# A graph network's attention stage: one-hots made by ScalarE, exponentials kept in PSUM, and sorting steps that read one half from PSUM

## Chip, core and metric

The kernel runs on one core of a Trainium2 chip. The metric is the device time of a run in microseconds, as the median of three runs; beside it stands one execution recorded by the hardware profiler. VectorE is called DVE in the profile, ScalarE ACT, GpSimd POOL, TensorE PE (with PEld for its weight loads) and SyncE SP.

## The reference

A graph has N = 12500 nodes with 128 features and E = 200000 edges, sorted by destination. Two layers follow one another: an edge-biased attention over each node's incoming edges, and three graph convolutions with batch norm.

```python
h = jnp.maximum(_layernorm(x, axis=-1), 0.0)
# attention, 8 heads of 16
q = (x @ Wq.T).reshape(N, H, C); k = ...; v = ...
scores = jnp.einsum('ehc,ehc->eh', q[dst], k[src]) / np.sqrt(C) + edge_attr @ We.T
seg_max = jax.ops.segment_max(scores, dst, num_segments=N)
ex = jnp.exp(scores - seg_max[dst])
denom = jax.ops.segment_sum(ex, dst, num_segments=N)
out = jax.ops.segment_sum(v[src] * (ex / denom[dst])[:, :, None], dst, num_segments=N)
...
x = x + out
h = jnp.maximum(_layernorm(x, axis=-1), 0.0)
# three times: h @ W, gather by src, times norm, segment_sum by dst, batch norm
x = x + graph_convolutions(h, src, dst)
```

## The kernel before, in words

A prologue normalises x, multiplies it by the three attention weights and writes q and the joined k and v rows to HBM tables (`q_d`, `kv_d`). A flag then chooses between a general path and `fast`, which runs here.

**Attention** (L885 to L1130) works on 106 tiles of 118 destination nodes. Each tile has a window of WE = 2048 edges, laid out as 128 partitions by JJ = 16. For each tile:

- 16 indirect DMAs of POOL (`gather`, L147, called for `kv`, with three buffers from pool `ga`) fetch the k and v rows of 128 edges each.
- A one-hot `oht` [128, 2048] (L1013, VectorE) compares the edges' local destinations with the partition number. TensorE multiplies its columns by `qt`, so that each edge gets its q row in PSUM (`qe`, L1019). VectorE multiplies by k (L1020, in four parts) and sums over each head (L1023).
- TensorE transposes the edge attributes (`et_p`, copied to `et` by ACT) and adds their bias (`sm`, L1036). Four scans (L1051, L1053, each twice), two scans across partitions (L1067, L1069) and small matmuls (L1058 to L1072) give each edge the maximum of its segment.
- ACT writes the exponentials into column C of `vals` in SBUF (L1081). VectorE multiplies the v rows by them (L1082).
- A second one-hot `oh` [128, 16, 118] (`one_hot`, L675 to L677, VectorE) serves as weights of the 16 matmuls that sum by destination into `acc` (L1089), which ACT copies out (L1090).

**Placing.** Between these parts runs a generator, `place_edges` (L680), which prepares the convolutions' layout. It sorts 106 rows of 2048 keys twice by a bitonic network. Each sort has 66 steps; each step is one minimum (L701) and one maximum (L702) over 1024 pairs, from one SBUF tile `A` to the other. Between and after the sorts stand other VectorE instructions over rows of up to 2048 elements (ranks, shifts by bits, masks). The generator stops at each `yield`. `go_on(1)` is called four times in a tile (L1025, L1063, L1073, L1084), so four stages of the generator are issued in each tile, from the group of tiles in which all edges have been loaded (tile 24) on. What is left is run after the last tile (L1129).

The lines above are the order in which the program is written. A scheduler then puts the instructions of each engine into one fixed queue, so that parts of two or three neighbouring tiles alternate. In the queue each instruction waits for its semaphores, and everything behind it waits too. The PSUM pools are `ps2` with two buffers (`qe`, `acc`) and `ps1` with one (`nb`, `et_p`, `sm`, `ends`): eight banks in all.

**Convolutions** (L1160 to L1400) come after attention. They use the placed layout: rows are taken from SBUF by one-hot matmuls, and the rest is gathered by POOL (`rows`).

Of the kernel before, what the change touches and what calls it, by code (L numbers as in the profile page):

```python
# [8 lines left out]
FP = mybir.dt.float32  # L9
BF = mybir.dt.bfloat16  # L10
I32 = mybir.dt.int32
AF = mybir.ActivationFunctionType
# [5 lines left out]
P = 128  # L18
D = 128
H = 8  # L20
# [28 lines left out]
def tile_gnn(ctx: ExitStack, tc: tile.TileContext, x, src, dst, ea, wqkvT, weT, w1, w2, w3, par, out):  # L49
# [608 lines left out]
    def fast():  # L658
# [16 lines left out]
        def one_hot(oh, dl):  # L675
            sh = list(oh.shape)
            nc.vector.tensor_tensor(oh, iota_f[:sh[0], :TN].unsqueeze(1).to_broadcast(sh),  # L677
                                    dl.unsqueeze(2).to_broadcast(sh), op=ALU.is_equal)

        def place_edges(rt, ps):  # L680
# [19 lines left out]
            def swap(lo, hi, lo2, hi2):  # L700
                nc.vector.tensor_tensor(lo2, lo, hi, op=ALU.min)  # L701
                nc.vector.tensor_tensor(hi2, lo, hi, op=ALU.max)  # L702

            def sort(turn):
                size = 2
                while size <= WE:
                    a, b = (x.rearrange("t (n z) -> t n z", z=size) for x in (A[turn], A[1 - turn]))
                    h = size // 2
                    swap(a[:, :, :h], a[:, :, h:][:, :, ::-1], b[:, :, :h], b[:, :, h:][:, :, ::-1])
                    yield  # L710
                    turn = 1 - turn
                    d = h // 2
                    while d:
                        a, b = (x.rearrange("t (n w d) -> t n w d", w=2, d=d) for x in (A[turn], A[1 - turn]))
                        swap(a[:, :, 0], a[:, :, 1], b[:, :, 0], b[:, :, 1])
                        yield
# [42 lines left out]
            nc.vector.tensor_scalar(sm[:, 3:4], sm[:, 2:3], float(OV), None, op0=ALU.is_gt)  # L759
            mb = ps.tile([P, 2, MG], FP, name="nb")  # L760
            nc.tensor.matmul(mb[0:1, 0, 0:1], sm[:, 3:4], ones[:NTT, 0:1], start=True, stop=True)
            yield
            nc.vector.tensor_scalar(slotted, mb[0:1, 0, 0:1], 0.0, None, op0=ALU.is_equal)

# [120 lines left out]
        with ExitStack() as s:  # L885
# [9 lines left out]
            ps2 = s.enter_context(tc.tile_pool(name="ps2", bufs=2, space=PSUM))  # L895
            ps1 = s.enter_context(tc.tile_pool(name="ps1", bufs=1, space=PSUM))

            wbd = once.tile([P, 4 * H], FP, name="wbd")
# [12 lines left out]
            nc.vector.tensor_scalar(shift[:, 0], iota_f, pid[:, 1:2], None, op0=ALU.is_equal)  # L911
            nc.vector.tensor_scalar(shift[:, 1], iota_f, pid[:, 2:3], None, op0=ALU.is_equal)
            NV = 2
            vals = [once.tile([P, JJ, H * (C + 1) + 1], FP, name=f"vals{i}") for i in range(NV)]
# [45 lines left out]
            def go_on(n):  # L960
                for _ in range(n if steps else 0):
                    next(steps, None)

            loaded = 0
            for t0 in range(0, NTT, NG):
                n = min(NG, NTT - t0)
                if t0 % MG == 0:
# [16 lines left out]
                    nc.vector.tensor_scalar(lf[:, 1, :mn], dw[:, :mn, 0], N + 1.0, None, op0=ALU.add)  # L984
                    nb = ps1.tile([P, 2, MG], FP, name="nb")
                    for k in range(2):
# [11 lines left out]
                for t in range(t0, t0 + n):  # L998
# [13 lines left out]
                    oht = wk.tile([P, WE], FP, name="oht")  # L1012
                    nc.vector.tensor_scalar(oht, dw_b, iota_q, None, op0=ALU.is_equal)  # L1013
                    ohv = oht.rearrange("a (p j) -> a p j", j=JJ)
                    qk = kv[:, :, :D]
                    for j in range(0, JJ, 4):
                        qe = ps2.tile([P, 4, D], FP, name="qe")
                        for k in range(4):
# [5 lines left out]
                                            qk.rearrange("p j (h c) -> p j h c", h=H), AX.X, ALU.add)  # L1024
                    go_on(1)  # L1025

# [45 lines left out]
                    nc.tensor.matmul(far[:, 1, :], r[:, 1, 1:], ident[:H, :H], start=True, stop=True)  # L1072
                    go_on(1)  # L1073
                    for k, j in ((0, 0), (1, JJ - 1)):
# [5 lines left out]
                    vh = va[:, :, :H * (C + 1)].rearrange("p j (h c) -> p j h c", h=H)  # L1080
                    nc.scalar.activation(vh[:, :, :, C], mx.rearrange("p h j -> p j h"), AF.Exp)  # L1081
                    nc.vector.tensor_tensor(vh[:, :, :, :C], kv[:, :, D:].rearrange("p j (h c) -> p j h c", h=H),  # L1082
                                            vh[:, :, :, C:].to_broadcast([P, JJ, H, C]), op=ALU.mult)
                    go_on(1)  # L1084
# [365 lines left out]
```

## Time and profile before

| what | value |
|---|---|
| median of three timed runs | 7355.95 us (7324.02 to 7399.03) |
| the profiled execution's own time | 6154.56 us |
| its span, first to last instruction | 6152.8 us |
| mean granted TensorE clock | 0.796 |
| busy: PE, PEld | 4406.0 (72%), 4115.5 (67%) us |
| busy: DVE, ACT, POOL | 3396.2 (55%), 1011.7 (16%), 4084.2 (66%) us |
| first and last gather of `kv` | about 148 and 2931 us |
| first and last sorting instruction (L701, L702) | about 744 and 1728 us |
| last placing instruction (L873) | about 2495 us |

A row of an instruction group reads: line, engine, operation, output<-inputs, count | busy us, mean ns of one | idle time of the engine just before them, and what ended it. "issue" means that nothing visible in the profile was waited for. A row of windows reads: start:end in us, length, then the busy time and count of PE, PEld, DVE, ACT and POOL, the granted clock, the DMA share and GB/s. A row of the timeline reads: start, length in us, engine, line, operation.

### The profile page before, as it was taken

The page shows a single profiled execution, that of the slowest core. Times are in us where ns is not written, and L with a number is a line of the kernel's source. Part 1 is how long each engine was busy: PE and PEld are TensorE (multiplying, and loading weights), DVE is VectorE, ACT ScalarE, POOL GpSimd, SP SyncE. Part 2 cuts the span into 40 slices and gives each one's busy share as a digit, 9 for nine tenths or more (in the row PEclk, how much of TensorE's full clock was granted, in tenths as well). Part 3 has the DMA queues.
Part 4 walks back from the last instruction along what each step waited for, and adds up shares of the span by engine and source line. Part 5 has one row for each costly group of instructions (what it writes and reads, how often), then busy time and mean ns, then how long its engine had stood idle before and what let it go on. Part 6 is the DMA issues. An engine that isn't in the chain of part 4 may idle for free. (4 is left out here: it accounts for less than half of the span.)

```text
span 6152.8 us, 80384 instructions
## 1 busy us (share of the span) xinstructions
PE 4406.0 (72%) x28564; PEld 4115.5 (67%) x28564; DVE 3396.2 (55%) x5972; ACT 1011.7 (16%) x2374; POOL 4084.2 (66%) x3617
## 2 busy tenths in 40 slices
PE   6676666666666665767487787877787787778777
PEld 2666655555566665666377777777777776777777
DVE  7566688887876677655243343353343344434344
ACT  3111111110111111111112122111121211112120
POOL 0777788888888888777266566636666664666663
PEclk9677766666676776767788888898888888888888
DMA  6555544433444444454588888878888887888888
GB/s 188 152 143 138 137 112 106 113 103 109 105 128 120 122 112 112 131 132 114 150 214 216 218 216 218 213 209 217 219 216 221 213 211 204 219 219 219 221 215 209
DMA packets 607714, 1051.07 MB, mean 171 GB/s; under 512 B 191227, under 2 KB 418491, under 8 KB 607201
## 3 DMA queue, kind: packets, MB, share of 16 engines
q1 hardware_dynamic: 464311, 695.85, 41.5%
q0 software_dynamic: 142608, 348.39, 23.9%
q8 instruction: 232, 3.80, 0.3%
q14 instruction: 175, 1.43, 0.1%
q10 hardware_dynamic: 388, 1.60, 0.1%
HBM read 773.19 MB, written 272.26 MB: 170 GB/s over the span
## 5 line engine op out<-in xcount | busy, mean ns | idle before, releaser
L148 POOL DMA_INDIRECT rows<-t_d,srcO x1908 | 1827.6, 958 | 1329.2 <-issue 560.2
L148 POOL DMA_INDIRECT kv<-kv_d,srcA x1696 | 2252.3, 1328 | 536.7 <-issue 484.3
L1249 DVE TENSOR_TENSOR oh<-nums,dlS 128x1888 f32<-128x1888 f32 x318 | 674.3, 2121 | 1527.2 <-PE zp L1255 1517.9
L1253 PE MATMUL zp<-oh,mr 128*128 128x118 f32 x6360 | 966.6, 319 | 567.5 <-DMA mr<-m 440.4
L1253 PEld LDWEIGHTS zp<-oh,mr 128*128 128x128 f32 x6360 | 925.5, 233 | 586.4 <-DMA mr<-m 348.7
L1019 PE MATMUL qe<-qt,oht 128*128 128x128 f32 x3392 | 841.4, 415 | 247.3 <-DVE kv L1020 110.7
L1224 PE MATMUL gp<-hs,go 128*117 128x128 f32 x7056 | 891.8, 281 | 125.8 <-DVE go L1221 69.8
L1019 PEld LDWEIGHTS qe<-qt,oht 128*128 128x128 f32 x3392 | 767.1, 310 | 289.7 <-issue 166.8
L1224 PEld LDWEIGHTS gp<-hs,go 128*117 128x117 f32 x7056 | 831.9, 184 | 165.1 <-issue 117.1
L1226 ACT COPY stage<-gp 117x512 f32<-117x512 f32 x1008 | 521.8, 532 | 1375.0 <-PE gp L1224 936.8
L1020 DVE TENSOR_TENSOR kv<-qe,kv 128x512 f32<-128x512 f32 x424 | 289.4, 685 | 678.8 <-DMA kv<-kv_d,srcA 536.8
L1089 PE MATMUL acc<-vals,oh 128*118 128x137 f32 x3392 | 539.8, 329 | 150.5 <-DVE vals L1082 150.0
L1089 PEld LDWEIGHTS acc<-vals,oh 128*118 128x118 f32 x3392 | 522.1, 225 | 171.6 <-DVE vals L1082 171.3
L1221 DVE TENSOR_SCALAR go<-gi,iota_q 128x468 f32<-128x468 uint8 x1008 | 427.8, 456 | 224.5 <-DMA gi<-gi_d 111.8
L1255 PE MATMUL zp<-oh,rows 128*128 128x118 f32 x3816 | 513.2, 288 | 0.2 <-DMA rows<-t_d,srcO 0.2
L1255 PEld LDWEIGHTS zp<-oh,rows 128*128 128x128 f32 x3816 | 492.2, 206 | 0.4 <-DMA rows<-t_d,srcO 0.4
L1058 PE MATMUL ends<-ident,mg 128*8 128x128 f32 x212 | 53.0, 343 | 344.4 <-DVE mg L1053 305.6
L1082 DVE TENSOR_TENSOR vals<-kv,vals 128x2048 f32<-128x2048 f32 x106 | 242.3, 2286 | 27.2 <-ACT vals L1081 26.8
L1058 PEld LDWEIGHTS ends<-ident,mg 128*8 128x8 f32 x212 | 11.7, 96 | 366.1 <-DVE mg L1053 298.8
L1023 DVE TENSOR_REDUCE sc<-kv 128x128 f32<-128x2048 f32 x106 | 240.8, 2272 | 0.0
L677 DVE TENSOR_TENSOR oh<-iota_f,dlA 128x1888 f32<-128x1888 f32 x106 | 224.0, 2113 | 5.0 <-PE acc L1089 5.0
L1036 PE MATMUL sm<-wbd,et 128*128 128x32 f32 x848 | 167.8, 351 | 45.0 <-DVE mg L1075 37.7
(242 smaller groups left out, 3648.1 us busy)
## 6 DMA issues: line engine op xcount, KB each, us to landing
m<-stage SPq DMA_DIRECT2D x252, 784.0 KB
mr<-m SPq DMA_DIRECT2D x318, 560.0 KB
dw_b<-dlb_d SPq DMA_DIRECT2D x106, 512.0 KB
gi<-gi_d SPq DMA_DIRECT2D x252, 204.8 KB
rows<-t_d,srcO POOLq DMA_INDIRECT x1908
kv<-kv_d,srcA POOLq DMA_INDIRECT x1696
ebx<-in_edge_attr_dram SPq DMA_DIRECT2D x106, 256.0 KB
mr<-m SPq DMA_DIRECT2D x318, 75.0 KB
```

What stands on the lines that cost most here:

```text
L148: nc.gpsimd.indirect_dma_start(out=o, out_offset=None, in_=table[:, :], in_offset=bass.IndirectOffsetOnAxis(ap=idx, axis=0))
L1019: nc.tensor.matmul(qe[:, k, :], ohv[:, :, j + k], qt, start=True, stop=True)
L1020: nc.vector.tensor_tensor(qk[:, j:j + 4, :], qe, qk[:, j:j + 4, :], op=ALU.mult)
L1023: nc.vector.tensor_reduce(sc.rearrange("p h j -> p j h"), qk.rearrange("p j (h c) -> p j h c", h=H), AX.X, ALU.add)
L1082: nc.vector.tensor_tensor(vh[:, :, :, :C], kv[:, :, D:].rearrange("p j (h c) -> p j h c", h=H), vh[:, :, :, C:].to_broadcast([P, JJ, H, C] ...
L1089: nc.tensor.matmul(acc, oh[:, j, :], va[:, j, :], start=(j == 0), stop=(j == JJ - 1))
L1221: nc.vector.tensor_scalar(go[:, :n], gv[:, a:a + n], iota_q, None, op0=ALU.is_equal)
L1224: nc.tensor.matmul(gp[:, i, :], go[:, i].rearrange("p t k -> p (t k)"), hs[:, g * SG + a + i, :], start=True, stop=True)
L1226: nc.scalar.copy(stage[:, a:a + n, :], gp[:, :n, :])
L1249: nc.vector.tensor_tensor(oh, nums.unsqueeze(1).to_broadcast(sh), dlS[:, t, :].unsqueeze(2).to_broadcast(sh), op=ALU.is_equal)
L1253: nc.tensor.matmul(zp[:, i, :], mr[:q, j, :], oh[:q, j, :], start=False, stop=False)
L1255: nc.tensor.matmul(zp[:, i, :], rows[:, j, :], oh[:, RC + j, :], start=False, stop=(j == JO - 1))
```

## The change

Five edits, all in attention and the placing that runs with it:

- `oht` and `oh` are made by ACT: Abs of the difference, then Relu(1 - x), which gives 1 where the difference is zero. `oh` takes one Abs for each of the 16 columns, because the bias is a value per partition.
- The exponentials go to PSUM (`ex`, a part of `sm`). VectorE's product reads them there, and ACT copies them to column C of `vals`.
- Each sorting step is cut in two halves. For each, ACT copies the upper elements to a PSUM bank (`hc`, one buffer), and after a `yield` the minimum and the maximum read them there.
- `go_on(2)` in place of `go_on(1)`, at all four places.
- PSUM: `sm` now has two buffers and also serves `nb`; `acc` has one and also serves the placing's `mb`; `hc` takes the bank that is free.

```diff
             def swap(lo, hi, lo2, hi2):
-                nc.vector.tensor_tensor(lo2, lo, hi, op=ALU.min)
-                nc.vector.tensor_tensor(hi2, lo, hi, op=ALU.max)
+                n, d = lo.shape[1:]
+                for k in range(2):
+                    cut = (slice(None), slice(k * n // 2, (k + 1) * n // 2)) if n > 1 else (
+                        slice(None), slice(None), slice(k * d // 2, (k + 1) * d // 2))
+                    hc = ps.tile([P, WE // 4], FP, name="hc")[:NTT].rearrange(
+                        "t (n d) -> t n d", n=max(1, n // 2))
+                    nc.scalar.copy(hc, hi[cut])
+                    yield
+                    nc.vector.tensor_tensor(lo2[cut], lo[cut], hc, op=ALU.min)
+                    nc.vector.tensor_tensor(hi2[cut], lo[cut], hc, op=ALU.max)
...
-                    swap(a[:, :, :h], a[:, :, h:][:, :, ::-1], b[:, :, :h], b[:, :, h:][:, :, ::-1])
-                    yield
+                    yield from swap(a[:, :, :h], a[:, :, h:][:, :, ::-1], b[:, :, :h], b[:, :, h:][:, :, ::-1])
...
-            mb = ps.tile([P, 2, MG], FP, name="nb")
+            mb = ps.tile([TN, H * (C + 1) + 1], FP, name="acc")
...
+            shared = [P, 2 * JJ + 2, H]
...
+            niota = once.tile([P, 1], FP, name="niota")
+            nc.vector.tensor_scalar(niota, iota_q, -1.0, None, op0=ALU.mult)
+
+            def where_zero(x):
+
+                nc.scalar.activation(x, x, AF.Relu, bias=ones[:, 0:1], scale=-1.0)
...
-                    nb = ps1.tile([P, 2, MG], FP, name="nb")
+                    nb = ps2.tile(shared, FP, name="sm")[:, :2, :MG]
...
-                    nc.vector.tensor_scalar(oht, dw_b, iota_q, None, op0=ALU.is_equal)
+                    nc.scalar.activation(oht, dw_b, AF.Abs, bias=niota[:, 0:1])
+                    where_zero(oht)
...
-                    go_on(1)
+                    go_on(2)
...
-                    sm = ps1.tile([P, JJ + 2, H], FP, name="sm")
-                    bias, far = sm[:, :JJ], sm[:, JJ:]
+                    sm = ps2.tile(shared, FP, name="sm")
+                    bias, far, ex = sm[:, :JJ], sm[:, JJ:JJ + 2], sm[:, JJ + 2:]
...
-                    nc.scalar.activation(vh[:, :, :, C], mx.rearrange("p h j -> p j h"), AF.Exp)
+                    nc.scalar.activation(ex, mx.rearrange("p h j -> p j h"), AF.Exp)
                     nc.vector.tensor_tensor(vh[:, :, :, :C], kv[:, :, D:].rearrange("p j (h c) -> p j h c", h=H),
-                                            vh[:, :, :, C:].to_broadcast([P, JJ, H, C]), op=ALU.mult)
-                    go_on(1)
+                                            ex.unsqueeze(3).to_broadcast([P, JJ, H, C]), op=ALU.mult)
+                    nc.scalar.copy(vh[:, :, :, C], ex)
+                    go_on(2)
                     oh = wk.tile([P, JJ, TN], FP, name="oh")
-                    one_hot(oh, dlA[:, t, :])
-                    acc = ps2.tile([TN, H * (C + 1) + 1], FP, name="acc")
+                    for j in range(JJ):
+                        nc.scalar.activation(oh[:, j, :], iota_f[:, :TN], AF.Abs, bias=dlA[:, t, j:j + 1], scale=-1.0)
+                    where_zero(oh)
+                    acc = ps1.tile([TN, H * (C + 1) + 1], FP, name="acc")
```

In the changed kernel the minimum and maximum stand on L709 and L710, the copy to `hc` on L707, the product on L1097, the Abs and Relu on L1027, L1103 and L925.

More of the change, by code (lines that the diff above doesn't have):

```diff
@@ L714, in sort @@
                         a, b = (x.rearrange("t (n w d) -> t n w d", w=2, d=d) for x in (A[turn], A[1 - turn]))
-                        swap(a[:, :, 0], a[:, :, 1], b[:, :, 0], b[:, :, 1])
-                        yield
+                        yield from swap(a[:, :, 0], a[:, :, 1], b[:, :, 0], b[:, :, 1])
                         turn = 1 - turn
@@ L759, in place_edges @@
             nc.vector.tensor_scalar(sm[:, 3:4], sm[:, 2:3], float(OV), None, op0=ALU.is_gt)
-            mb = ps.tile([P, 2, MG], FP, name="nb")
-            nc.tensor.matmul(mb[0:1, 0, 0:1], sm[:, 3:4], ones[:NTT, 0:1], start=True, stop=True)
+            mb = ps.tile([TN, H * (C + 1) + 1], FP, name="acc")
+            nc.tensor.matmul(mb[0:1, 0:1], sm[:, 3:4], ones[:NTT, 0:1], start=True, stop=True)
             yield
-            nc.vector.tensor_scalar(slotted, mb[0:1, 0, 0:1], 0.0, None, op0=ALU.is_equal)
+            nc.vector.tensor_scalar(slotted, mb[0:1, 0:1], 0.0, None, op0=ALU.is_equal)
             yield
@@ L1072, in fast @@
                     nc.tensor.matmul(far[:, 1, :], r[:, 1, 1:], ident[:H, :H], start=True, stop=True)
-                    go_on(1)
+                    go_on(2)
                     for k, j in ((0, 0), (1, JJ - 1)):
@@ L1080, in fast @@
                     vh = va[:, :, :H * (C + 1)].rearrange("p j (h c) -> p j h c", h=H)
-                    nc.scalar.activation(vh[:, :, :, C], mx.rearrange("p h j -> p j h"), AF.Exp)
+                    nc.scalar.activation(ex, mx.rearrange("p h j -> p j h"), AF.Exp)
                     nc.vector.tensor_tensor(vh[:, :, :, :C], kv[:, :, D:].rearrange("p j (h c) -> p j h c", h=H),
-                                            vh[:, :, :, C:].to_broadcast([P, JJ, H, C]), op=ALU.mult)
-                    go_on(1)
+                                            ex.unsqueeze(3).to_broadcast([P, JJ, H, C]), op=ALU.mult)
+                    nc.scalar.copy(vh[:, :, :, C], ex)
+                    go_on(2)
                     oh = wk.tile([P, JJ, TN], FP, name="oh")
-                    one_hot(oh, dlA[:, t, :])
-                    acc = ps2.tile([TN, H * (C + 1) + 1], FP, name="acc")
+                    for j in range(JJ):
+                        nc.scalar.activation(oh[:, j, :], iota_f[:, :TN], AF.Abs, bias=dlA[:, t, j:j + 1], scale=-1.0)
+                    where_zero(oh)
+                    acc = ps1.tile([TN, H * (C + 1) + 1], FP, name="acc")
                     for j in range(JJ):
```

## The prediction

> **What bounds the kernel now.** I read the page first, then tables of windows, the instruction groups of one window by form, and the timeline of a few microseconds. From the page, the two lines that the change concerns most:
>
> ```profile
> L148 POOL DMA_INDIRECT kv<-kv_d,srcA x1696 | 2252.3, 1328 | 536.7 <-issue 484.3
> L1082 DVE TENSOR_TENSOR vals<-kv,vals 128x2048 f32<-128x2048 f32 x106 | 242.3, 2286 | 27.2 <-ACT vals L1081 26.8
> ```
>
> The 1696 gathers of attention (16 for each of 106 tiles) take 1.328 us each and leave only "issue" between them, 0.30 us a time. They run from 148 to 2931 us, and 2252 + 537 = 2789 us is all of that stretch: POOL's gather queue sets the time of attention, waiting for nobody. The three convolutions (2990 us to the end) have other lines, and the change doesn't touch them. By stage (us, then PE, PEld, DVE, ACT, POOL busy, clock, DMA):
>
> ```profile
> 744.00:1214.00 470.00, 299.65 (x1523) 273.47 (x1524) 389.51 (x605) 59.01 (x158) 389.97 (x262) 0.69 0.42 111
> 1731.00:2495.00 764.00, 502.76 (x2559) 457.74 (x2557) 537.95 (x937) 99.63 (x256) 621.81 (x463) 0.71 0.45 117
> 2500.00:2930.00 430.00, 309.93 (x1584) 280.17 (x1584) 252.62 (x494) 56.43 (x155) 339.38 (x285) 0.70 0.49 126
> ```
>
> The first is a sort, the second the placing that follows both sorts, the third quiet. The quiet window makes 285/16 = 17.8 tiles in 430 us, 24.2 us a tile; the sort 16.4 tiles in 470 us, 28.7 us. The groups by form of 700 to 1700 us and 2500 to 2930 us show the same gather at two durations:
>
> ```profile
> L148 POOL DMA_INDIRECT kv<-kv_d,srcA x557 | 829.8, 1490 | 170.2 <-issue 163.2 <-DMA kv<-kv_d,srcA 4.3 <-DVE A L702 0.9
> ```
> ```profile
> L148 POOL DMA_INDIRECT kv<-kv_d,srcA x285 | 339.9, 1193 | 90.8 <-issue 78.6 <-DMA kv<-kv_d,srcA 10.3 <-DVE run L1069 0.9
> ```
>
> The timeline shows why (lines of PE, ACT and SP left out):
>
> ```profile
> 999.98 2.28 DVE L1082 TENSOR_TENSOR vals<-kv,vals 128x2048 f32<-128x2048 f32 x1
> ...
> 1001.16 1.92 POOL L148 DMA_INDIRECT kv<-kv_d,srcA  x1 [0.31 <-issue]
> ...
> 1004.63 0.95 POOL L148 DMA_INDIRECT kv<-kv_d,srcA  x1 [0.30 <-issue]
> 1004.84 0.69 DVE L1020 TENSOR_TENSOR kv<-qe,kv 128x512 f32<-128x512 f32 x1 [2.58 <-DMA kv<-kv_d,srcA]
> 1005.45 1.22 DVE L702 TENSOR_TENSOR A<-A 106x1024 f32<-106x1024 f32 x1
> 1005.88 1.59 POOL L148 DMA_INDIRECT kv<-kv_d,srcA  x1 [0.30 <-issue]
> 1006.58 2.28 DVE L1023 TENSOR_REDUCE sc<-kv 128x128 f32<-128x2048 f32 x1
> 1007.78 0.95 POOL L148 DMA_INDIRECT kv<-kv_d,srcA  x1 [0.30 <-issue]
> ```
>
> An undisturbed gather takes 0.945 us. One that starts under L1082 or L702, whose two inputs lie in SBUF, ends 0.8 us after that instruction ends (1003.08 after 1002.26; 1007.47 after 1006.67). L1020, with one input in PSUM, and the reduction L1023 leave gathers at 0.95. Over the whole trace I took, for each gather, the VectorE instruction running 0.1 us after its start: mean excess over 0.945 us is 1.58 us under L1082, 1.56 under L677, 0.82 to 0.87 under L701 and L702, 1.04 under L1013, but 0.03 under L1020 and 0.004 under L1023. The total is 650 us. By the instruction whose end freed the gather, L1082 has 177, L677 134, L701 with L702 101 and L1013 43: 455 us.
>
> **What the skill says.** "SBUF — State Buffer", section Who interferes with whom: a VectorE instruction with two SBUF inputs, or in a two-port mode, shuts out a GpSimd instruction that reads SBUF; with one SBUF input outside these modes it doesn't. The trace agrees (1.58 against 0.03 us). "ScalarE: Activation LUTs", section What ACT_TABLE_LOAD costs: about 0.28 us + 0.833 ns an element with a per-partition bias, back-to-back ones overlapping by 0.09 us. The trace's `hg` (118 elements, bias and scale pointers) takes 0.482 us, which agrees; the long Abs and Relu are in no row of it. "TensorE: Matmul & The Clock Gate", Part 1: the clock rises with activity. The trace goes 0.70 in attention to 0.88 in the denser convolutions.
>
> **The change, part by part.**
>
> One-hots: VectorE loses L1013 (1.28 us) and L677 (2.11) per tile. ACT gains, by the skill's price as estimates: Abs 2048 = 1.99, Relu 1.99, 16 Abs of 118 at 0.285 = 4.6, Relu 1888 = 1.85: 10.4 us. Abs and Relu add no table loads (59 in both built programs).
>
> Exponentials: L1082 keeps its 2.29 us but has one SBUF input left. ACT gains a copy of 128 elements, 0.3 us (`cm`, 136 elements: 0.303). ACT then has 56.43/17.8 = 3.2 us + 10.7 = 13.9 us in a quiet tile.
>
> Sort: 132 steps of 1.205 + 1.212 us become 264 halves of one ACT copy of 512 (0.59 us, as `et`) and two tensor_tensors of 512 with a PSUM input (0.67 us, L1020 has 0.685 alone and 0.64 in a pair). VectorE: 264 x 1.34 = 354 us against 319. `hc` has one buffer, so each copy waits for the pair before it, and each pair for its copy: a ring of two engines, with the other ACT work (five to seven Abs, a Relu of 2 us) queued between copies in the built order.
>
> Eight steps a tile: a half is a step, so the sort's pace stays about four full steps a tile. The built program starts the sort at ACT's tile 22, ends the second at tile 58 and the placing at tile 73. The placing's own instructions are as before (136 us of VectorE, summed from the trace) but in 15 tiles instead of 29. `acc` drops to one PSUM buffer, `sm` gains one: the matmul L1089 of the next tile waits for ACT's copy of `acc`, 0.27 us (L1090), small if ACT is on time.
>
> Sum over attention's gathers, 148 to 2931 us:
>
> - Before the sort, now 25.1 tiles in 596 us. A quiet tile is 16 x 1.25 = 20.0 us + 4.2 us excess; the three disarmed instructions had (177 + 134 + 43)/106 = 3.3 us of that, so 20.9 remains, and I take 21. After: 25 x 21 = 525.
> - Sorts, now 987 us for 34.1 tiles. After, 36 tiles: VectorE has 36 x 11.0 (810.5 us busy in 700 to 1700, less sort, L677 and L1013, over 34.8 tiles) + 354 + 20 between the sorts = 770 us. This exceeds POOL's 36 x 21 = 756. VectorE is 81% busy in 700 to 1700 us; I assume 82% in its new ring: 940 us. ACT would be at 36 x 13.9 + 264 x 0.59 = 656 us.
> - Placing, now 764 us for 28.9 tiles. After, 15 tiles: 15 x 21 + 70 us of gathers held by placing instructions (some 66 two-input ones of 1.1 to 1.5 us and the two-port ones, at half their length squared over 1.25 us) = 385.
> - Quiet rest, now 436 us for 17.9 tiles. After, 30 x 21 = 630.
>
> Together 2480 us against 2783: 303 us less, a profiled execution of some 5850 us. Its own time was 6154.6 us (span 6152.8), while the median of the timed runs is 7356, 1201 us more, which no view of this profile explains. I subtract in absolute terms: 7356 - 303 = 7053, say 7055. If it scaled, it would be 6994.
>
> **Rivals.**
>
> Gathers stay the only bound (the ring is hidden): sorts 36 x 21.5 = 774, together 2314, 469 us less: 6887. For: DVE's 770 us fits. Against: no slack.
>
> Quiet tiles don't follow POOL: PE has 309.93/17.8 = 17.4 us a tile, 83% of 21, in order, and the timed runs may run at a lower clock than 0.70. At 0.5 everywhere PE would need 17.4 x 0.70/0.5 = 24.4 us. Then quiet tiles gain nothing, 61 x 24.5 against 43 now, total 2807 before (596 and 436 become 615 and 441) and 612 + 940 + 390 + 735 = 2677 after: 130 less, 7226.
>
> Slower: the ring goes serial. If no other work of either engine overlaps, a half costs 0.59 + 1.34 + other DVE 396/264 = 1.5 + other ACT 500/264 = 1.9 + two handoffs of 0.15 (estimate) = 5.6 us, 1480 us for the sorts, 3020 in all: 237 us more, 7593. It decides where a half exceeds (2783 - 525 - 385 - 630)/264 = 4.7 us; my forecast is 3.6. Against it: the built order puts other VectorE work between most pairs.
>
> **How the numbers follow.** The forecast's case 0.55, gathers alone 0.17, quiet tiles bound by PE 0.13, a ring at 4.4 to 5.0 us (no net change) 0.08, slower 0.07. A measurement of this kernel can tell about 1%, 74 us. Faster by over 1%: 0.85; within: 0.08; slower: 0.07. The range runs from the gathers-alone case, a little below, 6850, to past the PE case, 7270; the forecast's own range is 6960 to 7150.
>
> **What would show it.** Right: the gather's mean near 1.0 us and no excess under L1097 (the old L1082), L709 and L710; quiet tiles near 21 us; ACT near 14 us a quiet tile; sort halves near 3.6 us with VectorE waiting for `hc` copies. Wrong: gathers still held under instructions with a PSUM input; POOL waiting for DMA or for `vals` in quiet tiles; PE waiting for `oht` or `oh` from ACT; sort halves above 4.7 us.

## The result and the profile after

| | median of the timed runs | profiled execution |
|---|---|---|
| before | 7371.95 us (7324.02 to 7399.03, four runs) | 6154.56 us |
| after | 7952.85 us (7950.59 to 7971.63, four runs) | 7950.59 us, span 7948.7 us |

The ratio is 1.0801, with a 95% interval of 1.0738 to 1.0864: slower by 8%, where 7055 us and a gain were forecast. The page of the changed kernel, four groups (the second number after the bar is the mean in ns, then the idle time before them and what ended most of it):

```profile
L148 POOL DMA_INDIRECT kv<-kv_d,srcA x1696 | 1677.9, 989 | 1816.3 <-DVE vals L1097 1052.7
L1103 ACT ACTIVATE oh<-iota_f,dlA 128x118 f32<-128x118 f32 x1696 | 512.4, 381 | 6.3 <-issue 6.3
L1097 DVE TENSOR_TENSOR vals<-kv,sm 128x2048 f32<-128x2048 f32 x106 | 241.5, 2278 | 12.8 <-ACT sm L1096 9.3
L707 ACT COPY hc<-A 106x512 f32<-106x512 f32 x264 | 156.3, 592 | 308.0 <-DVE A L710 219.8
```

A gather now takes 0.989 us instead of 1.328, so 574 us of POOL's work are gone. But its idle time rose from 537 to 1816 us. Before, POOL waited for nobody; now it waits 1053 us for L1097, the product that reads a tile's `kv` buffer last. ACT's Abs (second row) hardly wait; its copies for the sort (fourth) do. The product itself (third) waits 9 us in all for the exponentials that ACT makes.

One fact has to come first, since no number below can be read without it: the program before takes about 6155 us on some chips and about 7330 us on others. By its time, its profile at the start came from a chip of the first kind; the timed comparison and the profile of after came from the second kind. In the experiments the program before took 6149 to 6168 us on four chips, called prompt here, and 7279 to 7378 us on two, called late. Each of these six chips was used in one group of runs only, so "chip" may also mean the condition that it was in at that time. The two profiles above can't be subtracted from each other. The partner of the first on a prompt chip is the run `e5_after_again` (span 5795.1 us), that of the second on a late chip `e16_before_fourth` (span 7287.5 us), both below.

Windows of after on the late chip (start:end, length, then busy time of PE, PEld, DVE, ACT, POOL, clock, DMA share, GB/s): before the sorts, sorts, placing, the quiet rest, and most of the convolutions:

```profile
150.00:1023.00 873.00, 421.07 (x2148) 384.86 (x2148) 293.64 (x823) 334.57 (x789) 393.79 (x415) 0.66 0.39 99
1023.00:2326.00 1303.00, 666.82 (x3304) 598.52 (x3304) 749.39 (x1523) 652.51 (x1337) 580.13 (x594) 0.64 0.33 91
2326.00:2644.00 318.00, 186.30 (x995) 170.11 (x996) 241.55 (x405) 163.49 (x352) 208.55 (x168) 0.68 0.40 99
2644.00:3639.00 995.00, 563.15 (x2855) 508.78 (x2853) 348.30 (x821) 421.99 (x914) 494.73 (x520) 0.67 0.37 101
3750.00:7850.00 4100.00, 2695.67 (x18378) 2568.94 (x18378) 1249.20 (x1698) 598.52 (x1151) 1783.09 (x1863) 0.79 0.61 160
```

The same stages of the program before on a late chip:

```profile
148.00:828.00 680.00, 417.60 (x2114) 377.76 (x2115) 368.25 (x875) 85.36 (x309) 447.27 (x401) 0.69 0.51 125
828.00:1811.00 983.00, 609.27 (x3074) 553.66 (x3074) 805.77 (x1233) 117.63 (x319) 817.74 (x542) 0.67 0.42 110
1811.00:2605.00 794.00, 505.40 (x2589) 459.72 (x2587) 541.54 (x940) 99.39 (x255) 621.43 (x464) 0.71 0.43 113
2605.00:3081.00 476.00, 307.07 (x1603) 278.19 (x1603) 254.91 (x498) 57.48 (x160) 332.12 (x289) 0.70 0.44 116
3200.00:7200.00 4000.00, 2709.90 (x18288) 2579.84 (x18287) 1250.77 (x1681) 592.50 (x1132) 1788.83 (x1870) 0.79 0.62 163
```

And of after on a prompt chip, sorts, quiet rest and convolutions:

```profile
701.00:1565.00 864.00, 630.08 (x3304) 577.87 (x3304) 749.87 (x1522) 648.90 (x1337) 597.33 (x600) 0.75 0.54 139
1851.00:2560.00 709.00, 535.84 (x2928) 491.18 (x2928) 364.56 (x858) 430.17 (x941) 498.04 (x523) 0.78 0.57 143
2650.00:5700.00 3050.00, 2390.95 (x18316) 2319.56 (x18315) 1232.13 (x1694) 591.73 (x1149) 1779.88 (x1859) 0.88 0.83 215
```

Divide each length by its tiles (gathers of `kv` in the window over 16) and the picture is a table of us per tile:

| stage | before, prompt | after, prompt | before, late | after, late |
|---|---|---|---|---|
| before the sorts | 23.8 | 21.6 | 27.1 | 33.7 |
| sorts | 29.1 | 23.1 | 29.0 | 35.1 |
| placing | 26.5 | 27.5 | 27.4 | 30.2 |
| quiet rest | 24.2 | 21.8 | 26.5 | 30.7 |

In each window the busy times of DVE, ACT and POOL in after hardly depend on the chip: in the sorts DVE has 749 us on both, ACT 653 and 649. Only the length differs, 1303 against 864 us. What grows is waiting. Attention, from the first gather to the last, takes 2933 us before and 3489 after on late chips: 556 of the 661 us by which the two spans differ. The convolutions, which the change doesn't touch, have 80 more (4085 and 4165 us from the first to the last `rows` gather). These 80 belong to the chips: on another late chip before has 4163 (`e7_before_sum_twice`).

### The profile page after: what moved, and what is told of

Read it like the earlier page. It is cut to its first block, busy times and chain, and to the rows that moved or that the text cites. A ratio compares the mean times of both kernels' runs of the same rounds, so it can differ in the third digit from the quotient of the medians.

```text
span 7948.7 us, 82553 instructions
## 1 busy us (share of the span) xinstructions
PE 4729.6 (60%) x28564; PEld 4370.8 (55%) x28564; DVE 3083.6 (39%) x6025; ACT 2242.7 (28%) x4758; POOL 3508.5 (44%) x3617
## 5 line engine op out<-in xcount | busy, mean ns | idle before, releaser
L148 POOL DMA_INDIRECT kv<-kv_d,srcA x1696 | 1677.9, 989 | 1816.3 <-DVE vals L1097 1052.7
L1242 PE MATMUL gp<-hs,go 128*117 128x128 f32 x7056 | 1058.3, 308 | 767.9 <-issue 553.1
L1271 PE MATMUL zp<-oh,mr 128*128 128x118 f32 x6360 | 1065.0, 339 | 616.6 <-DMA mr<-m 350.0
L1242 PEld LDWEIGHTS gp<-hs,go 128*117 128x117 f32 x7056 | 959.0, 208 | 853.0 <-issue 663.5
L1271 PEld LDWEIGHTS zp<-oh,mr 128*128 128x128 f32 x6360 | 1020.0, 252 | 637.8 <-issue 332.1
L1244 ACT COPY stage<-gp 117x512 f32<-117x512 f32 x1008 | 523.6, 533 | 2293.2 <-PE gp L1242 883.6
L1107 PE MATMUL acc<-vals,oh 128*118 128x137 f32 x3392 | 572.4, 341 | 299.4 <-ACT vals L1099 169.3
L1103 ACT ACTIVATE oh<-iota_f,dlA 128x118 f32<-128x118 f32 x1696 | 512.4, 381 | 6.3 <-issue 6.3
L1051 PEld LDWEIGHTS sm<-wbd,et 128*128 128x128 f32 x848 | 139.6, 243 | 266.4 <-DVE con L1007 139.5
L1097 DVE TENSOR_TENSOR vals<-kv,sm 128x2048 f32<-128x2048 f32 x106 | 241.5, 2278 | 12.8 <-ACT sm L1096 9.3
L707 ACT COPY hc<-A 106x512 f32<-106x512 f32 x264 | 156.3, 592 | 308.0 <-DVE A L710 219.8
```

Source lines behind the costliest of these rows:

```text
L148: nc.gpsimd.indirect_dma_start(out=o, out_offset=None, in_=table[:, :], in_offset=bass.IndirectOffsetOnAxis(ap=idx, axis=0))
L1051: nc.tensor.matmul(bias[:, 4 * k:4 * k + 4, :].rearrange("p j h -> p (j h)"), et[:, k, :], wbd, start=True, stop=True)
L1103: nc.scalar.activation(oh[:, j, :], iota_f[:, :TN], AF.Abs, bias=dlA[:, t, j:j + 1], scale=-1.0)
L1107: nc.tensor.matmul(acc, oh[:, j, :], va[:, j, :], start=(j == 0), stop=(j == JJ - 1))
L1242: nc.tensor.matmul(gp[:, i, :], go[:, i].rearrange("p t k -> p (t k)"), hs[:, g * SG + a + i, :], start=True, stop=True)
L1244: nc.scalar.copy(stage[:, a:a + n, :], gp[:, :n, :])
```

## What is different on a late chip, and why it hurts the kernel after

The convolutions are the same code in both programs, so they show the chip alone: about 3120 us on prompt chips, about 4080 to 4165 on late ones, at a clock of 0.79 instead of 0.88 and a DMA share of 0.61 to 0.62 instead of 0.83. A packet of the gathers (4096 bytes) takes 250 to 274 ns on both, so the DMA engines aren't what is late. What is late is TensorE's handover: I paired each of the 1008 copies of L1244 (L1226 before) with the matmul group that it waits for. On prompt chips a copy starts 0.04 us (median) after both TensorE's recorded end and ACT's previous instruction, and none over 2 us. On late chips 188 to 207 of them start over 2 us later, 3.9 to 4.6 us on average, 804 to 868 us together (seven traces). The handovers of other engines aren't late. Measured in the same way in attention of after, none of ACT's 106 exponentials (after VectorE), none of POOL's 103 refills (after the product) and none of VectorE's 264 minimums (after ACT's copy to `hc`) is over 2 us late, and of the 106 products (after ACT's exponentials) one, by 2.3 us.

Whether TensorE really ends later than its (modelled) records say, or its signal travels late, the trace doesn't tell. TensorE's own matmuls also start late there with no wait in sight: before L1242 it idles 767.9 us in after, 553.1 of them "issue", against 130.2 us in all on a prompt chip. And the late traces lack many signals, of all engines: of TensorE's, VectorE's and ACT's, 9642 of 10809, 4296 of 5743 and 2572 of 3518 are in the trace of after. A wait whose signal can't be matched has "remote" as its releaser, so releasers are less sure there than starts and ends.

What this does to attention is seen in the timeline of after, quiet rest, late chip (start, length, engine, line; the idle time before it in brackets):

```profile
3133.48 2.28 DVE L1097 TENSOR_TENSOR vals<-kv,sm 128x2048 f32<-128x2048 f32 x1
...
3136.02 0.95 POOL L148 DMA_INDIRECT kv<-kv_d,srcA  x1 [12.14 <-DVE vals L1097]
...
3138.62 3.92 PE L1107 MATMUL acc<-vals,oh 128*118 128x137 f32 x32
...
3142.05 0.29 DVE L1093 TENSOR_TENSOR mg<-sc,mg 128x128 f32<-128x128 f32 x1
...
3142.37 0.50 PE L1001 MATMUL sm<-lf,shift 128*128 128x4 f32 x4
...
3157.38 0.27 ACT L1108 COPY att<-acc 118x137 f32<-118x137 f32 x1 [15.69 <-remote]
3157.55 0.39 ACT L1096 ACTIVATE sm<-mg 128x128 f32<-128x128 f32 x1
3157.87 3.21 ACT L1103 ACTIVATE oh<-iota_f,dlA 128x118 f32<-128x118 f32 x11
3158.84 0.23 DVE L1007 TENSOR_TENSOR con<-sm,lf 128x4 f32<-128x4 f32 x2 [16.49 <-remote]
...
3160.12 2.28 DVE L1097 TENSOR_TENSOR vals<-kv,sm 128x2048 f32<-128x2048 f32 x1
...
3162.67 0.95 POOL L148 DMA_INDIRECT kv<-kv_d,srcA  x1 [6.89 <-DVE sc L1053]
```

The sums of a tile are recorded as done at 3142.5. ACT's copy of them starts at 3157.38. Behind it in ACT's queue stand the next tile's exponentials (L1096), whose input L1093 was ready at 3142.34, and then 16 Abs and a Relu for `oh`. VectorE is held at the same time: its L1007 reads what L1001 wrote, which is recorded as done at 3142.87, and starts only at 3158.84. The product L1097 needs the exponentials, ready at 3157.94, and stands behind L1007 in VectorE's queue, so VectorE's own wait for TensorE ends last here. When the product ends, at 3162.40, the buffer is free and POOL starts 0.27 us later, after 6.89 us of waiting (the row names an earlier VectorE instruction; the product's end is the one that fits in time). The copy of `acc` is over 2 us late in 67 of 106 tiles there, 676 us together; before on a late chip, 15 of 106 (176 us); on a prompt chip, in no tile. VectorE's L1090, which reads TensorE's results directly, is over 2 us late in 30 tiles (294 us), before on a late chip in 5, on a prompt chip in none. So TensorE hands over late far more often under after than under before, on the same kind of chip.

What POOL sees of this is the ring of the three `kv` buffers: from a tile's first gather to the end of the product that frees its buffer (latency), and from that end to the first gather that fills it again (slack). Computed from the traces:

| run | latency, us | a third of it | slack, median us | refilled within 0.5 us |
|---|---|---|---|---|
| before, prompt | 59.6 | 19.9 | 20.0 | 2% of tiles |
| after, prompt | 61.4 | 20.5 | 5.5 | 32% |
| before, late | 65.2 | 21.7 | 17.6 | 19% |
| after, late | 96.7 | 32.2 | 0.27 | 84% |

In after on a late chip nearly every buffer is refilled as soon as it is free, so POOL has lost the pace. (That a third of the latency, 32.2 us, is near the 3489/106 = 32.9 us of a tile says no more than this: three buffers that never lie free give one tile in each third of the latency, whatever makes it long.) In the program before the buffers lie free for 17.6 us even there, and its latency grows by 6 us against 35 in after.

A full ring can have two causes. Either VectorE waits for rows, because there are too few buffers, or the rows lie ready and wait for VectorE. The waits tell which. Of after (late), then of before (late), then of after (prompt), each over attention (us in total, times, longest):

```profile
POOL kv L148 <- DVE vals L1097: 1052.7, 69, 49.3
ACT att L1108 <- remote: 582.7, 37, 37.3
POOL kv L148 <- issue: 473.5, 1534, 2.8
...
DVE mg L1090 <- remote: 293.8, 24, 20.8
DVE kv L1035 <- remote: 283.1, 29, 35.4
DVE sc L1053 <- remote: 224.0, 13, 39.6
...
DVE con L1007 <- remote: 140.5, 13, 18.5
...
DVE kv L1035 <- DMA kv<-kv_d,srcA: 19.2, 4, 7.6
```
```profile
DVE kv L1020 <- DMA kv<-kv_d,srcA: 305.0, 96, 6.6
...
POOL kv L148 <- DVE vals L1082: 174.7, 16, 31.4
```
```profile
DVE kv L1035 <- DMA kv<-kv_d,srcA: 395.3, 126, 11.0
...
POOL kv L148 <- DVE vals L1097: 134.7, 30, 13.3
```

Waiting for the product is 1053 us for POOL in the first, 175 and 135 in the others. But VectorE waits 19 us for rows there, 305 and 395 in the others, and 941 us on four lines that all read a result of TensorE. The DMA packets, whose records are complete, say the same without releasers: between the landing of a quarter tile's rows and their multiplication by q lie 29.0 us on average in after (late), 9.1 in before (late) and 6.2 in after (prompt). So on a late chip the rows are early and wait for VectorE, and VectorE waits for TensorE, which in its turn waits for VectorE and ACT: the exchange between these three sets the pace, and POOL's 1053 us follow from that. By these records a lack of `kv` buffers isn't what holds this program back.

## The experiments

**The two kernels again, chip by chip.** The first question was whether the profiled execution or the timed runs of before were the exception. Kernel before, unchanged:

> The kernel before, unchanged, to see whether the profiled execution of 6154.6 us is typical beside a median of 7356. If that execution was an exception, this profile shows about 7350 us, with the convolutions at some 4200 us (as in the changed kernel's profile) and attention at 24 to 30 us a tile. If the timed runs have a cost outside the profile, it shows about 6150 us again. Ratio to the kernel before: 1.00 either way.

Measured: 6164.16 us against 6167.55, ratio 0.9997 (0.9989 to 1.0006), span of the profile 6169.1. The time of the first profile is the normal one on that chip. The kernel after, unchanged:

> The changed kernel, unchanged, beside the kernel before on the chip of this call. The three parts alone gained 2.8, 3.8 and 1.3% where the kernel before took 6168 us. If the loss of 8% belongs to the changed kernel itself (a conflict of its parts), it is slower here too: ratio above 1.03, quiet tiles above 28 us. If the loss belongs to the condition in which the first comparison ran (7350 us for the kernel before), then where the kernel before takes about 6160 us the ratio is 0.93 to 0.97, quiet tiles take 20 to 22 us, and its convolutions take 3200 us.

Measured: 5798.73 us (5789.24 to 5802.89) against 6164.01, ratio 0.9405 (0.9389 to 0.9422). On a prompt chip the change gains 6%. The page's gather row there:

```profile
L148 POOL DMA_INDIRECT kv<-kv_d,srcA x1696 | 1701.7, 1003 | 714.4 <-issue 470.4
```

Before was run twice more, for its trace on further chips:

> The kernel before, for a profile in the condition of this call. If this chip is one where it takes about 7370 us: convolutions near 4160 us and attention near 2900 us, its quiet tiles slower than 24.2 us with POOL sometimes waiting for a kv buffer, its sort tiles unchanged at 29 us (theory S: POOL, held by the sort, hides the late TensorE there). If it takes about 6165 us, all as in its first profile.

Measured: 6163.35 us, prompt.

> The kernel before, for a profile in the condition of this call. Where it takes 7370 us: convolutions near 4160 us, sort tiles near 29 us as ever, quiet tiles 26 to 31 us with POOL waiting for kv buffers there. Where it takes 6165 us: as in its first profile.

Measured: 7289.32 us, late; it is the trace of before that the tables above use. Its gather row shows about the length of a gather on prompt chips (1.309 against 1.328 us there) and 178 us more idle time than the 542 of the run before it:

```profile
L148 POOL DMA_INDIRECT kv<-kv_d,srcA x1696 | 2220.0, 1309 | 719.7 <-issue 490.2
```

**Parts of the change alone, prompt chips.** The forecasts of the next three runs count on a program before of about 7370 us, so on the prompt chip that they got none of them is met or refuted. After with both one-hots back on VectorE:

```diff
-                    nc.scalar.activation(oht, dw_b, AF.Abs, bias=niota[:, 0:1])
-                    where_zero(oht)
+                    nc.vector.tensor_scalar(oht, dw_b, iota_q, None, op0=ALU.is_equal)
...
-                    for j in range(JJ):
-                        nc.scalar.activation(oh[:, j, :], iota_f[:, :TN], AF.Abs, bias=dlA[:, t, j:j + 1], scale=-1.0)
-                    where_zero(oh)
+                    one_hot(oh, dlA[:, t, :])
```

> The changed kernel with both one-hots back on VectorE. Theory 1 (the one-hots on ACT stand in ACT's fixed queue between a tile's gathers and the product L1097 that frees its kv buffer, so that POOL waits for buffers): most of the 580 us comes back, 7250 to 7450 us, and POOL waits little for L1097. Rival (the sorting ring between ACT and VectorE, or the single acc buffer, is the cause): 7800 to 7950 us.

Measured: 5993.18 us, ratio 0.9717 (0.9701 to 0.9734). Before with nothing but that edit, the other way round:

> The kernel before with only the two one-hots made by ACT. Theory 1: 7700 to 7950 us, with quiet tiles above 30 us and POOL waiting for L1097's counterpart. Rival (sorting ring or acc): about 7250 us, below the kernel before, since two of the blocking instructions are gone.

Measured: 5930.57 us, 0.9621 (0.9605 to 0.9637). Before with only the sort's halves, `go_on(2)` and one buffer for `acc`:

```diff
-                nc.vector.tensor_tensor(lo2, lo, hi, op=ALU.min)
-                nc.vector.tensor_tensor(hi2, lo, hi, op=ALU.max)
+                n, d = lo.shape[1:]
+                for k in range(2):
...
-                    go_on(1)
+                    go_on(2)
...
-                    acc = ps2.tile([TN, H * (C + 1) + 1], FP, name="acc")
+                    acc = ps1.tile([TN, H * (C + 1) + 1], FP, name="acc")
```

> The kernel before with only the sorting halves read from PSUM, eight placing stages a tile, and acc in one PSUM buffer. Theory 1: 7250 to 7380 us, since the gathers are freed from the sort's two-input instructions and ACT has little else to do. Rival (sorting ring or acc): 7700 to 7950 us.

Measured: 6085.07 us, 0.9868 (0.9852 to 0.9885). Then after with one of the two one-hots back, the wide one (`oht`, the first half of the first diff) and the narrow ones (`oh`, the second half):

> The changed kernel with the wide one-hot oht back on VectorE. Theory A (a tile's ring passes through ACT's fixed queue, where a copy that waits for TensorE holds up the one-hots that TensorE needs next): where the kernel before takes 7370 us, half or more of the 580 us comes back, 7500 to 7700 us; where it takes 6165 us, some 80 us slower than the changed kernel, since a blocking instruction is back. Rival (acc or sm decides): 7900 to 8000 us, or 5800 to 5880 us.

> The changed kernel with the narrow one-hots oh back on VectorE (6.5 us of ACT less per tile). Theory A: 7500 to 7750 us where the kernel before takes 7370 us; where it takes 6165 us, some 100 us slower than the changed kernel, 5880 to 5950 us. Rival (acc or sm decides): 7900 to 8000 us where the kernel before takes 7370 us.

Measured: 5834.33 us, 0.9468 (0.9444 to 0.9492), and 5883.99 us, 0.9541 (0.952 to 0.9562). So on prompt chips each one-hot that ACT takes over is a gain: 0.6 points of the time of before for `oht`, 1.4 for `oh`, 3.1 for both. The 36 us for `oht` are less than the 80 of theory A and lie in its rival's range.

**A longer latency on a prompt chip.** One rival theory put the loss down to `acc`'s single PSUM buffer. After, with `acc` given two and `sm` (with `nb` and `mb`) one:

```diff
-                    nb = ps2.tile(shared, FP, name="sm")[:, :2, :MG]
+                    nb = ps1.tile(shared, FP, name="sm")[:, :2, :MG]
...
-                    sm = ps2.tile(shared, FP, name="sm")
+                    sm = ps1.tile(shared, FP, name="sm")
...
-                    acc = ps1.tile([TN, H * (C + 1) + 1], FP, name="acc")
+                    acc = ps2.tile([TN, H * (C + 1) + 1], FP, name="acc")
```

> The changed kernel with two PSUM buffers for acc and one for sm, as before the change. Theory B (one buffer for acc makes TensorE wait for ACT's copy, which itself waits for a late TensorE): where the kernel before takes 7370 us, 7500 to 7750 us; where it takes 6165 us, up to 60 us faster than the changed kernel. Theory A: within 1.5% of the changed kernel in both conditions, or slower, since the exponentials now hold the only sm buffer.

Measured: 6910.48 us, 1.1211 (1.1185 to 1.1237). Theory B's 60 us of gain on a prompt chip did not come, but the edit also takes a buffer from `sm`, so it doesn't test `acc` alone, and on a late chip it wasn't run. It does show, without any late signal (its convolutions are as on any prompt chip), what a longer ring does. Its latency is 99.9 us, a third is 33.3, and attention takes (3650 - 150)/106 = 33.0 us a tile. 97% of the buffers are refilled within 0.5 us. Its waits from 150 to 3500 us:

```profile
DVE kv L1035 <- DMA kv<-kv_d,srcA: 1387.4, 335, 12.2
POOL kv L148 <- DVE vals L1097: 1035.7, 74, 25.8
```

The second line is nearly that of after on a late chip (1052.7 us), but the first is its opposite: here VectorE waits 1387 us for rows, and uses them 1.1 us after they land. This is the case in which the buffers themselves set the pace. It isn't the case of the late chip, where VectorE waits 19 us for rows. A gather in its quiet rest takes 0.950 us and saves nothing.

**A longer latency on purpose.** Each tile's 16 summing matmuls issued twice (the sum is started anew, so only time is added), in before and in after:

```diff
                     for j in range(JJ):
                         nc.tensor.matmul(acc, oh[:, j, :], va[:, j, :], start=(j == 0), stop=(j == JJ - 1))
+                    for j in range(JJ):
+                        nc.tensor.matmul(acc, oh[:, j, :], va[:, j, :], start=(j == 0), stop=(j == JJ - 1))
```

> The kernel before with the 16 summing matmuls of each tile issued twice (the second pass starts the sum anew, so the result is the same): TensorE gets about 5.1 us more per tile and signals the end of the sum later. Theory S (the kernel before has slack against a late TensorE: a kv buffer lies free for a median of 20 us before POOL refills it, so POOL still sets the tile): at most 1.5% slower, 0 to 90 us. Rival (both kernels pay alike for a late TensorE): as much as the changed kernel with the same edit, about 300 us.

> The changed kernel with the same doubled sum. Theory S (the faster gathers have used up the slack: 32% of gathers that refill a kv buffer start within 0.5 us of its release, the median wait is 5.5 us, and ACT's queue now stands between TensorE and the one-hots that TensorE needs): 300 us or more slower than the changed kernel, 6100 us or more, so that most of its gain of 365 us is gone, though TensorE's 17.4 + 5.1 us a tile are under the kernel before's 24.2. Rival (TensorE's work counts only where it exceeds the tile's time): about 22.5 us in quiet tiles, 60 to 120 us slower, 5860 to 5920 us.

Both ran on a late chip. Measured: before 7578.63 us, 1.026 (1.0218 to 1.0302); after 8226.58 us, 1.1144 (1.1101 to 1.1187). The same two on another chip, which proved late as well:

> The kernel before with the doubled sum, hoped for in the condition where it takes 6165 us without. Theory S (a kv buffer there lies free for a median of 20 us, so a later TensorE is hidden): at most 60 us slower, below 6230 us. Rival (it pays by TensorE's work): 200 us or more slower.

> The changed kernel with the doubled sum. Theory S: more than 150 us slower than the changed kernel's 5799 us, 5950 us or more, so that at least 40% of its gain is gone. Rival (TensorE counts only where its own 22.5 us exceed the tile): 5830 to 5900 us.

Measured: 7451.64 us, 1.0257 (1.0214 to 1.0299), and 8084.83 us, 1.1106 (1.106 to 1.1151). Against after's own 1.0801 this edit costs after 3.1 to 3.4%, and before 2.6%. So on a late chip before doesn't hide longer TensorE work either: theory S allowed it 90 us, and it paid 201 and 173. These four don't tell the theories apart. With the edit before's latency is 78.2 us, and 41% of its buffers are refilled at once: it has come near its ring too.

**One-hots on VectorE on a late chip.** The edit of the first diff of this group:

> The changed kernel with both one-hots on VectorE, hoped for where the kernel before takes 7370 us. Theory A (one-hots on ACT put ACT's queue into the ring): 7250 to 7500 us, most of the 580 us comes back. Theory S alone (any kernel whose gathers are quick pays): 7650 to 7900 us. Where the kernel before takes 6165 us: 5990 us again.

Measured: 7639.77 us (7615 to 7660) against 7278.74, 1.0492 (1.045 to 1.0534). The same edit that costs 3.1 points on prompt chips gives back 3.1 of the 8.0 here. That is neither "most of the 580 us" of theory A nor, by 10 us, inside its rival's range: the one-hots on ACT matter on a late chip, but they are less than half of the loss. The copy of `acc` is over 2 us late in 36 tiles instead of 67, the latency is 89.3 us, and a quiet tile 26.9 us, about what before needs (26.5). The sort's tiles stay at 35.7 us against before's 29.0. The waits of its sort window:

```profile
POOL kv L148 <- DVE vals L1096: 459.1, 26, 38.3
ACT hc L707 <- DVE A L710: 260.6, 145, 5.6
```

ACT waits 261 us there for the halves' `hc` ring, and POOL 459 us for the product. That points to the sort for most of what is left of the loss: 33.3 tiles at 6.7 us more are 223 of the 340 us by which attention is longer than that of before. But the tiles ahead of the sorts, where no half runs, take longer too:

```profile
150.00:953.00 803.00, 436.72 (x2180) 390.77 (x2180) 375.85 (x886) 93.76 (x341) 442.07 (x427) 0.68 0.43 111
```

These 26.7 tiles take 30.1 us each against 27.1 in before, 80 us together, which the sort can't explain.

**The other parts alone**, to settle that on a late chip. Before with the exponentials in PSUM only (two buffers for `sm`, `acc` keeps its two, `mb` moved to `et_p`):

```diff
-                    nc.scalar.activation(vh[:, :, :, C], mx.rearrange("p h j -> p j h"), AF.Exp)
+                    nc.scalar.activation(ex, mx.rearrange("p h j -> p j h"), AF.Exp)
...
-                                            vh[:, :, :, C:].to_broadcast([P, JJ, H, C]), op=ALU.mult)
+                                            ex.unsqueeze(3).to_broadcast([P, JJ, H, C]), op=ALU.mult)
+                    nc.scalar.copy(vh[:, :, :, C], ex)
```

> The kernel before with the exponentials in PSUM, sm in two buffers (it serves nb too) and acc still in two; sort and one-hots as before. Both theories: gathers freed from L1082, 100 to 180 us faster where the kernel before takes 6165 us; where it takes about 7300 us, 0 to 150 us faster, because no new exchange with ACT is put into the ring.

The same with the one-hots on ACT, that is the whole change but the sort:

> The same, and the one-hots on ACT; sort as before. Theory R (the sorting ring costs the rest of the loss): where the kernel before takes about 7300 us, 200 to 350 us slower than it at most, with sorting tiles near 29 us and quiet tiles near 30 us; where it takes 6165 us, 5780 to 5850 us, as fast as the whole change or nearly. Rival (the two ACT parts hurt only together): within 60 us of e17 in the first condition.

And the sort's halves alone again:

> The kernel before with only the sorting halves, eight stages a tile and acc in one buffer. Theory R: where the kernel before takes about 7300 us, sorting tiles of 33 to 36 us instead of 29 and 100 to 300 us slower. Rival: sorting tiles at 26 to 29 us, no slower than the kernel before. Where it takes 6165 us: 6085 us again.

They landed on a prompt chip. Measured: 5974.53 us, 0.9715 (0.9699 to 0.9731); 5747.58 us, 0.9348 (0.9332 to 0.9364), below its forecast of 5780 to 5850; 6069.13 us, 0.9865 (0.9847 to 0.9884). What follows is for prompt chips only. One-hots and exponentials multiply exactly: 0.9621 x 0.9715 = 0.9347, measured 0.9348. With the sort's halves on top it would be 0.922, and after is 0.9405. The halves (with `go_on(2)` and the single buffer of `acc`) gain 1.3% alone and lose 0.6% on top of the rest. The version without them has more slack (median 11.7 us, 7% refilled at once) and is the fastest of all kernels on these chips. POOL's row of its quiet rest, 1950 to 2500 us:

```profile
L148 POOL DMA_INDIRECT kv<-kv_d,srcA x411 | 415.6, 1011 | 135.3 <-issue 117.5 <-DMA kv<-kv_d,srcA 8.4 <-DVE vals L1090 7.2
```

Of 135 us idle only 7 are waits for the product. How it fares on a late chip wasn't measured.

## Why the prediction was wrong, step by step

**Gathers freed: right.** The prediction named means near 1.0 us and no excess under the instructions with a PSUM input. Measured 0.989 and 1.003 us, and 0.952 to 0.954 in the quiet rest; the mean excess of gathers that start under L1097, L709 and L710 is 0.00, 0.01 and 0.07 us (late), and 0.00, 0.00 and 0.09 (prompt). "SBUF — State Buffer", section Who interferes with whom, holds: one SBUF input outside the two-port modes leaves GpSimd alone.

**ACT's new work: right.** 13.9 us a quiet tile were forecast; 430.17 us for 32.6 tiles are 13.2. The price in "ScalarE: Activation LUTs", What ACT_TABLE_LOAD costs, was used as 0.285 us for an Abs in a row; eight in a row took 2.36 us, 0.295 each. (The prediction's row of `hg` has 118 partitions and 128 elements, not 118 elements; by the price that is 0.01 us.)

**The sum against the profiled execution: right on the kind of chip that it was made for.** Forecast 2480 us of attention, measured 5795.1 us of span with attention at 2410 (150 to 2560); forecast a profiled execution of 5850, measured 5799. Sizes: quiet tile 21.8 us (21), before the sorts 21.6 (21), a half 864/264 = 3.27 us (3.6), 37.4 tiles in the sorts (36). A placing tile took 27.5 us instead of 25.7, but there were 10.4 of them, not 15. That the sum came within 3% is partly luck: the sorts and the placing were 76 and 99 us shorter than forecast, the other two stages 26 and 79 us longer.

**The step that failed: "I subtract in absolute terms: 7356 - 303 = 7053".** The text before it says that 1201 us lie between the profiled execution and the median of the runs and that no view explains them. It then gave these 1201 us to nothing in particular, and kept for the timed runs the structure of the profile, in which POOL sets the tile and a `kv` buffer lies free for 20 us. The term that was put at nothing without a reason is how the change acts under those 1201 us. On the chips of the timed runs TensorE hands over late. VectorE waits 941 us for TensorE's results and 19 us for rows, POOL waits 1053 us for the product, and attention takes 3489 us where before takes 2933. Two of the prediction's own signs of being wrong came: POOL waiting for the product in quiet tiles (275 us from 2650 to 3600 us), and halves above 4.7 us.

**The rival with the right place and the wrong size.** "Quiet tiles don't follow POOL" tied the unexplained time to PE's throughput at half its clock, 24.5 us a tile and a gain of 130 us. The granted clock is 0.67 there, and PE is busy 563 of 995 us: by these records throughput isn't the bound. The waits for TensorE's results are, and tiles take 30 to 35 us. Priced so, it would have been the slower rival. (Its "61 x 24.5" is a slip: the sums after it use 25 and 30 tiles.)

**The ring of the sort.** Its threshold was 4.7 us a half. On a late chip a half takes 1303/264 = 4.94 us, but not by the mechanism that I priced (two engines without overlap): ACT's waits for L710 are 220 us of those 1303. With the one-hots back, the sort's tiles are as slow.

**What stays open.** Of the 8.0 points, 3.1 hang on the one-hots on ACT, as `e15_onehots_on_dve_again` shows. By which path isn't shown. It isn't the product's direct wait for the exponentials (9 us in all); in the timeline above ACT's queue and VectorE's were held together. That most of the rest is the sort's halves is argued from the tiles of 35.7 us and wasn't shown, since none of the parts came to run alone on a late chip; some of the rest arises before any half runs. No run takes the late handovers away, so that they make the loss is read from the traces. Why they are late on some chips, and why more of them are late under after than under before, I can't say. More `kv` buffers don't fit into SBUF beside the rest and weren't tried; with rows that lie ready for 29 us I would not expect a gain from them on a late chip.

## What to carry to other kernels

Before shortening the engine that sets the pace, ask what sets it next: the time that a freed buffer waits for its refill says how far away that is. When that time is gone, look at the reader. If the reader waits for data, the buffers are the bound, as in `e9_acc_two_sm_one`; if data lie ready, the stage behind is, as in after on a late chip, though the filling engine shows the same thousand microseconds of waiting in both. And if the timed runs and the profiled execution differ by a fifth, the profile shows another condition: forecast for both, with the chance of each.

## What the runs showed of the hardware that I had not expected

One program, two times: 6149 to 6168 us on four chips, 7279 to 7378 on two, 19% apart, each kind repeating within 1.4%. The late kind shows it in the identical convolutions (clock 0.79 against 0.88, a fifth of the copies of TensorE's results over 2 us late, about 4 us on average) while DMA packets, VectorE's and ScalarE's instructions keep their lengths and the other engines' handovers that were paired stay prompt. And a change can be worth -6% on one kind and +8% on the other.
